# Two layers on one core: the parameters' preparation put behind the first Gram matrix, and one unit's work instead of two beside the second

## The chip, the cores and the metric

The kernel runs on one core of a Trainium2 chip. The metric is the device time of one execution in microseconds (us): here the median of three runs. Everything is in float32.

## What is computed

The input x has the shape 16 x 32 x 128 x 128 (samples, channels, rows, columns). Two residual layers follow one another:

```python
x = x + _L0_conv_ref(_gn(x), Wq, Wkv, Wout, bout)      # attention over channels
x = x + _L1_conv_ref(_gn(x), pn_g, ..., k4_bb)         # four small networks on 8 x 8 windows
```

Layer 0 normalises groups of channels (`_gn`), joins eight samples to 256 channels of 16384 positions, projects them to queries, keys and values, and lets channels attend to channels: `sim` is a product over all positions, so that it follows from the 256 x 256 Gram matrix of x. Once the attention matrix is known, the whole layer is one linear map of the channels at each position. There are two groups of eight samples, so two Gram matrices and two maps.

Layer 1 normalises again, cuts 8 x 8 windows and puts them through four `_fastkan` networks:

```python
ln = _layernorm(x, ln_g, ln_b)
basis = jnp.exp(-((ln[..., None] - GRID) / DENOM) ** 2)       # 8 Gaussians
flat = basis.reshape(*basis.shape[:-2], -1)
return flat @ ws.T + jax.nn.silu(x) @ wb.T + bb
```

Two of them run along a window's columns and rows, one on its positions, and the fourth on their sum.

## The kernel before, in words

**Stages.** The work has three stages on the time axis.

1. *Gram matrix of group 0, then of group 1* (`gram_load`, `gram_turn`, `gram_sum`, L610 to L694). Each needs all positions of eight samples. `gram_load` brings x in 16 loads of 2 MB (8 for each group), half of each issued by SP's queue and half by ACT's (L636), into three pairs of buffers for group 0 and two pairs for group 1. A load waits until the turns on the earlier load of its buffers are done (L627). `gram_turn` has 64 steps: two vector transposes on DVE each (L657), four steps to a load, into two alternating tiles R. `gram_sum` has 64 steps: 16 matmuls each, four for each of four pieces b (L683; the trace shows 32 records a step, two to a matmul). Turn m writes the tile that sum m-2 read. Below, "load m", "turn m" and "sum m" count from 0; turn 32 and sum 32 are the first of group 1, turn 63 and sum 63 the last.
2. *Attention* (L696 to L973), once for each group: a chain of about 50 short steps that goes back and forth between PE, DVE and ACT and ends in the map `pt` and some columns. Attention 0 stands beside the second Gram matrix, attention 1 beside the first units. Its products use the projections' weights, which Pool's queue brings in (`projections`, L589 to L605: eight DMAs of 256 KB, then a copy on Pool, L604).
3. *64 units* of 128 x 1024 elements each: 32 of group 0, then 32 of group 1. For a unit, `layer0_norm` applies the map (L1003), takes the mean out (L1018) and takes the variance (L980); `rows_norm` scales (L1051, L1056, L1060, L1064); SP moves the result into a second layout, `move` (L1097), which `norm_a` needs; `norm_a` and `norm_b` normalise for the networks (L436 to L1122), `scale` multiplies (L1139), `seed` takes the first exponentials on ACT (L1148 to L1156), `ladder` makes the other Gaussians, 7 products of 128 x 2048 on DVE for each of two halves a and b (L1168), and `products` multiplies them with the weights (L436, L1204, L1323). `keep` stores a unit's layer-0 result and `load` brings the next x, which has a single buffer (1 MB, both units of a pair, L993).

**What sets the order.** PE, ACT, DVE and SP run their instructions strictly in the order in which the program issues them. That order is made while the program is built, by a small planner (`Flow.run`, L144). Each task is a generator that asks for an engine with a guessed duration (`step("DVE", 0.6)`), for buffers, or for another task's result (`yield "get", ...`). For the steady state the planner has a fixed cyclic order for each engine (`ORDER`, L53 to L74), in which each entry names a task, its step and how many units it lags. While that order isn't able to go on, or where it would be later, tasks outside it (attention, Gram, parameters, projections) are let in by their modelled time. Among these, three names go first where times are equal (`FIRST`, L76). Until the second Gram matrix is found, only units with a number below `AHEAD` may be started by the cyclic order (L77, L199, L208): units 0 and 1 before the change.

**`parameters`** (L486 to L584) prepares the constants of layer 1. Its first step is Pool's: 32 DMAs of 4.5 KB (`st_a`, into a raw tile `sz`, L501), and 8 of 18 KB (`wt_b`, L507) mixed with 16 of 2 KB (`st_b`, L511). Then come 14 steps on DVE and three transposes on PE (L541): L515 to L528 need the columns loaded at the top (L304 to L308), L550 to L570 need `st_a` (its two halves one after the other), L572 needs `wt_b`, L576 and L577 need `st_b`. `rows_norm` of unit 0 waits for all of it (L1047), and so do the seeds' columns and the products' weights. Pool issues its DMAs in order, at the top of the program first the 40 small ones of the columns (L304 to L308), then `parameters`, then `projections`.

Of the kernel before, what the change touches and what calls it, by code (L numbers as in the profile page):

```python
# [73 lines left out]
}  # L74

FIRST = {"attention", "projections", "parameters"}  # L76
AHEAD, UNTIL = 2, ("gram", 1)  # L77
TURNS = 7


def step(engine, us, *take, lag=None):


    return engine, us, take, LAG if lag is None else lag


class Flow:
# [22 lines left out]
    def put(self, key, value, late=0.0):  # L110
        self.found[key] = (value, self.now + late)
# [128 lines left out]
def conv_preact_kernel(  # L240
# [75 lines left out]
    def column():  # L316
        used[0] += 1
        return vec[:, used[0] - 1 : used[0]]

    eps, one, ones_n = column(), column(), column()  # L320
# [123 lines left out]
    def layers():  # L444
        with ExitStack() as es:
# [39 lines left out]

            def parameters():  # L486

                raw, = yield step("POOL", 40.0, "sz")
                back_t = raw[:, 0:384].rearrange("p (k q m) -> p k q m", k=3, q=4)
                st_a = [  # L490
                    raw[:, 384 + k * NT * 16 : 384 + (k + 1) * NT * 16].rearrange("p (t n) -> p t n", t=NT)
# [97 lines left out]
            def projections():  # L589

                qk, wv_raw, wo, low, mid = yield step("POOL", 5.0, "ad_r", "z", "sz", "att", "u")
                qk = qk.rearrange("p l t w -> p (l t w)").rearrange("p (i k n) -> p i k n", i=2, k=KK)
                wq, wk = qk[:, 0], qk[:, 1]
                wv_ = mid[:, 0:1024].rearrange("p (h k c) -> p h k c", h=PAIRS, k=KK)
                wv_raw = wv_raw.rearrange("p (h m s) -> p h m s", h=PAIRS * KK, s=2)
                wo = wo.rearrange("p (h n) -> p h n", h=PAIRS)
                for s in range(2):
                    nc.gpsimd.dma_start(out=wq[s::2], in_=wqT[s * 64 : (s + 1) * 64])
                    nc.gpsimd.dma_start(out=wk[s::2], in_=wkT[s * 64 : (s + 1) * 64])
                for e in range(2):  # L600
                    nc.gpsimd.dma_start(out=wv_[64 * e : 64 * e + 64], in_=wv[:, e::2])
                    nc.gpsimd.dma_start(out=wo[64 * e : 64 * e + 64], in_=woT[:, e::2])
                yield step("POOL", 3.0)
                nc.gpsimd.tensor_copy(wv_raw, wv_.rearrange("p h k (s m) -> p (h k) m s", s=2))  # L604
                put("projections", (wq, wk, wv_raw, wo, low, mid))  # L605
# [4 lines left out]
            def gram_load():  # L610

                half = S // LOAD
                turn = [m % 3 if m < half else m % 2 for m in range(NBP * half)]
                for m in range(NBP * half):
                    if m == 0:
                        ad, yy, u0, u1, d, sd = yield step("SP", 2.6, "ad", "yy", "u", "u", "d", "sd", lag=-2.6)
                        flat4 = lambda t: t.rearrange("p l t w -> p (l t w)")
                        xs = [  # L620
                            [t.rearrange("p (g n) -> p g n", g=4) for t in pair]
                            for pair in ((flat4(ad), flat4(yy)), (u0, u1), (flat4(d), flat4(sd)))
                        ]
                    else:
                        old = [i for i in range(m) if turn[i] == turn[m]]
                        if old:
                            yield "get", ("turned", 4 * old[-1] + 3)  # L627
                        yield step("SP", 2.6, lag=-2.6)
                    bp, j = divmod(m, half)
                    for queue in (nc.sync, nc.scalar):  # L630
                        if queue is nc.scalar:
                            yield step("ACT", 2.6)
                        for r in (0, 1) if queue is nc.sync else (2, 3):
                            for k in range(KK):
                                at = j * LOAD + r * 512
                                queue.dma_start(  # L636
                                    out=xs[turn[m]][k][32 * r : 32 * r + 32],
                                    in_=x_groups[bp, k, :, :, at : at + 512],
                                )
                    put(("xs", m), xs[turn[m]], fl.moved(6.5, 2.6))  # L640

            def gram_turn():


                turned = yield step("DVE", 0.2, "R", "R")
                turned = [t[:, 0 : 4 * KK * (P + 1)].rearrange("p (b n) -> p b n", b=4) for t in turned]
                for t in turned:
                    nc.vector.memset(t[:, :, P], 1.0)
                for m in range(NBP * STEPS):
                    xr = yield "get", ("xs", m // 4)  # L650
                    if m >= 2:
                        yield "get", ("summed", m - 2)
                    yield step("DVE", 1.3)
                    o = slice(128 * (m % 4), 128 * (m % 4) + 128)
                    for k in range(KK):
                        at = k * (P + 1)
                        nc.vector.transpose(  # L657
                            turned[m % 2][:, :, at : at + P].rearrange("p b (g c) -> p g b c", g=4), xr[k][:, :, o]
                        )
                    put(("turned", m), None)  # L660
                    if m == STEPS - 1:
                        give("d")
                        give("sd")
                    put(("xT", m), turned[m % 2])
# [468 lines left out]
            def scale(name, n):  # L1133
                rb = yield "get", (name, "rb", n)
                v = yield "get", (name, "v", n)
                for i in range(2):
                    o = slice(i * RB, (i + 1) * RB)
                    yield step("DVE", 1.14, lag=0.0 if i == 0 else None)
                    TT(v[:, o], v[:, o], flat(rb[i]), ALU.mult)  # L1139
                    give("Y")  # L1140
                put((name, "scaled", n), v)
# [231 lines left out]
            one = lambda name, task: [(name, 0, task)]  # L1373
            every = lambda name, task, units=N: ((name, n, task(n)) for n in range(units))
            with tc.manual_schedule(engines=IN_ORDER):
                fl.run(
                    [
                        one("parameters", parameters()),
                        one("projections", projections()),
                        (("attention", bp, attention(bp)) for bp in range(NBP)),  # L1380
                        one("gram_load", gram_load()),
                        one("gram_turn", gram_turn()),
                        one("gram_sum", gram_sum()),
                        ((f"products_{k}", n, (pair_a if k == "a" else pair_b)(n)) for k, n in both),
                        every("evict_a", evict_a),
                        every("evict_z", evict_z),
                        every("result", result),
                        every("again", again),
                        every("scale_b", lambda n: scale("b", n), N + BACK),
                        every("scale_a", lambda n: scale("a", n)),  # L1390
                        ((f"seed_{k}", n, seed(k, n, par_a if k == "a" else par_b)) for k, n in both),
                        every("norm_b", norm_b, N + BACK),
                        every("norm_a", norm_a),
                        every("silus", silus, N + LATE),
                        every("move_back", move_back),
                        every("move", move),
                        every("rows_norm", rows_norm),
                        every("keep", keep),
                        every("layer0_norm", layer0_norm),
                        every("load", load),  # L1400
                        every("store", store),
                        ((f"ladder_{k}", n, ladder(k, n)) for k, n in both),
                    ],
                    N + max(BACK, LATE),
                )

    layers()


# [78 lines left out]
```

## Time and profile before

| | us |
|---|---|
| median of three runs (2882.24 to 2889.74) | 2883.42 |
| the profiled execution | 2885.47 |
| its span, first to last instruction | 2883.70 |
| PE busy in the span | 2748.3 (95%) |
| DVE busy in the span | 2685.2 (93%) |
| ACT busy in the span | 2518.4 (87%) |
| turn 0 begins (first L657) / sum 0 begins (first L683) | 14.98 / 17.18 |
| sum 31 ends (first Gram matrix) | 118.78 |
| sum 63 ends (second Gram matrix) | 234.25 |
| first ladder product, unit 0 (first L1168) | 246.54 |
| first ladder product of unit 1 / of unit 2 | 295.2 / 360.02 |
| from then on, a unit takes | 39.5 to 39.6 |

A timeline row of the trace gives the start and the length in us, the engine, the line, the operation, the tiles written and read, and in brackets how long the engine was idle before it and what ended that. A row "by stage" gives a window, its length, each engine's busy time with the number of instructions, the clock granted to TensorE as a share of full speed, the mean share of the DMA engines, and the GB/s that they moved. Busy times of PE are modelled, since matmuls overlap.

### The profile page before, as it was taken

Reading aid. Unit: us, or ns where it says so; the run is one execution under the profiler, and the core shown is the slowest. Engines: PE = TensorE matmul, PEld = TensorE weight load, DVE = VectorE, ACT = ScalarE, POOL = GpSimd, SP = SyncE. Lnnn points to the kernel's source line nnn. Section 1 sums busy time; section 2 is a strip of 40 time slices with the busy share of each in tenths; the row PEclk is TensorE's granted clock in tenths of the full one; section 3 lists DMA queues with packets and bytes.
Section 4 is the critical chain, followed back from the end, with each engine's and each line's share of the span. In section 5 each row is a group of like instructions: output and inputs, shape, how many; then the busy total and the mean of one; then the engine's idle time right before and its main releaser. Section 6 shows DMA issues by size and latency. Waiting matters only on the chain.

```text
span 2883.7 us, 100690 instructions
## 1 busy us (share of the span) xinstructions
PE 2748.3 (95%) x45955; PEld 1092.4 (38%) x45955; DVE 2685.2 (93%) x1793; ACT 2518.4 (87%) x2035; POOL 53.8 (2%) x109
## 2 busy tenths in 40 slices
PE   6899899999999999999999999999999999999985
PEld 6774333333333333333333333333333333333321
DVE  4557799999999999999999999999999999999986
ACT  0018699999999999999999999999999999999973
POOL 5200000000000000000000000000000000000000
PEclk9899999999999999999999999999999999999987
DMA  9660233333333333333333333333333333333311
GB/s 223 165 171 28 78 101 107 109 115 104 98 113 99 117 114 110 104 107 109 115 106 94 115 98 117 114 110 104 108 108 115 110 95 111 101 114 113 103 52 38
DMA packets 206152, 311.04 MB, mean 108 GB/s; under 512 B 24480, under 2 KB 156064, under 8 KB 205728
## 3 DMA queue, kind: packets, MB, share of 16 engines
q1 hardware_dynamic: 192512, 285.29, 33.5%
q10 hardware_dynamic: 9504, 16.85, 2.4%
q8 instruction: 362, 5.93, 0.9%
q0 software_dynamic: 3712, 2.46, 0.4%
q14 instruction: 62, 0.51, 0.1%
HBM read 103.18 MB, written 67.11 MB: 59 GB/s over the span
## 4 chain that ended last, share of the span: by engine, by line
PE 64%; DVE 21%; issue 6%; DMA 4%; ACT 3%; SPq 1%; DVEq 0%; POOL 0%; ACTq 0%; POOLq 0%
PE X L436 25%; DVE u L1168 15%; PE X L1204 10%; PE Y L1003 8%; PE Y L1018 4%; PE Y L436 4%; PE X L1323 4%; PE X L683 3%; DVE yc L1139 3%; PE Y L980 2%; PE Y L1122 2%; DVE yy L1056 2%; DMA sz<-in_w 1%; DMA col<-in_cols 1%; SPq L1240 1%
## 5 line engine op out<-in xcount | busy, mean ns | idle before, releaser
L1168 DVE SCALAR_TENSOR_TENSOR u<-R,u 128x2048 f32<-128x2048 f32 x910 | 2042.6, 2285 | 39.0 <-ACT u L1153 15.2
L436 PE MATMUL X<-u,wt_a 32*32 32x512 f32 x16384 | 658.9, 600 | 8.5 <-DVE u L1168 3.6
L436 PE MATMUL X<-u,wt_b 32*32 32x512 f32 x16896 | 640.3, 608 | 14.8 <-ACT u L1153 9.4
L436 PEld LDWEIGHTS X<-u,wt_a 32*32 32x32 f32 x16384 | 302.2, 103 | 282.6 <-issue 138.4
L436 PEld LDWEIGHTS X<-u,wt_b 32*32 32x32 f32 x16896 | 225.6, 103 | 384.0 <-issue 195.6
L1139 DVE TENSOR_TENSOR yc<-yc,Y 128x1024 f32<-128x1024 f32 x260 | 305.2, 1214 | 7.7 <-PE Y L1122 4.8
L1148 ACT ACTIVATE u<-yc,vec 128x2048 f32<-128x2048 f32 x130 | 258.5, 1988 | 29.7 <-DVE yc L1139 25.9
L1003 PE MATMUL Y<-x,pt 128*128 128x512 f32 x512 | 238.4, 609 | 34.7 <-DVE yc L1139 34.7
L1114 ACT ACTIVATE yc<-Y 128x1024 f32<-128x1024 f32 x260 | 250.5, 1017 | 16.6 <-PE Y L436 16.6
L1156 ACT ACTIVATE R<-yc,vec 128x2048 f32<-128x2048 f32 x130 | 259.4, 1995 | 1.3 <-DVE u L1168 0.3
L1150 ACT ACTIVATE R<-yc,vec 128x2048 f32<-128x2048 f32 x130 | 258.8, 1990 | 0.0
L1117 ACT ACTIVATE u<-yc 128x2048 f32<-128x2048 f32 x130 | 247.5, 1904 | 5.1 <-DVE u L1168 2.5
L1153 ACT ACTIVATE u<-u 128x2048 f32<-128x2048 f32 x130 | 247.1, 1901 | 0.0
L683 PE MATMUL X<-R 128*64 128x193 f32 (+3 forms) x2048 | 156.7, 313 | 39.0 <-DVE R L657 38.2
L982 ACT ACTIVATE lr<-Y,vec 128x512 f32<-128x512 f32 (+1 forms) x194 | 131.5, 678 | 45.4 <-PE Y L980 45.4
L683 PEld LDWEIGHTS X<-R 128*64 128x64 f32 x2048 | 145.1, 142 | 56.7 <-DVE R L657 40.8
L1003 PEld LDWEIGHTS Y<-x,pt 128*128 128x128 f32 x512 | 92.7, 191 | 184.7 <-issue 93.7
L980 PE MATMUL Y<-u,e 128*32 128x512 f32 x1040 | 140.5, 606 | 3.3 <-ACT u L1117 3.3
L1232 ACT ACTIVATE ad<-X,col 128x1024 f32<-128x1024 f32 x128 | 134.1, 1097 | 0.9 <-PE X L436 0.7
L1018 PE MATMUL Y<-xh,c 128*128 128x512 f32 x256 | 128.4, 625 | 1.3 <-DVE yc L1139 1.3
L983 ACT ACTIVATE lr<-lr 128x512 f32<-128x512 f32 (+1 forms) x194 | 122.3, 631 | 6.2
L1204 PE MATMUL X<-sd,silu_a 64*64 64x512 f32 x1024 | 126.3, 608 | 0.0
(210 smaller groups left out, 2468.0 us busy)
## 6 DMA issues: line engine op xcount, KB each, us to landing
xh<-xh SPq DMA_DIRECT2D x128, 512.0 KB
d<-yy SPq DMA_DIRECT2D x512, 128.0 KB
ad_r<-ad SPq DMA_DIRECT2D x512, 128.0 KB
x<-in_x SPq DMA_DIRECT2D x32, 1024.0 KB
out<-xh SPq DMA_DIRECT2D x256, 128.0 KB
u<-in_x SPq DMA_DIRECT2D x28, 256.0 KB
u<-in_x ACTq DMA_DIRECT2D x28, 256.0 KB
ad<-in_x SPq DMA_DIRECT2D x14, 256.0 KB
```

Source lines behind the costliest of these rows:

```text
L436: MM(dst(to, g_), lhsT=wt[32 * g_ : 32 * g_ + 32, :], rhs=rhs(g_, (to - turn[g_]) % 4), start=start, stop=stop,)
L683: MM(g[64 * q : 64 * q + 64, k, lo:hi], lhsT=t[:, b, at : at + 64], rhs=t[:, b, lo:hi], start=first, stop=last,)
L1003: MM(xp[:, u, :], lhsT=pts[bp][:, k, kk * P : (kk + 1) * P], rhs=xr[:, k, u * 512 : (u + 1) * 512], start=k == 0, stop=k == KK - 1,)
L1114: ACT(v[:, i * RB : (i + 1) * RB], flat(yt[i]), AF.Identity)
L1117: ACT(sq, v, AF.Square)
L1139: TT(v[:, o], v[:, o], flat(rb[i]), ALU.mult)
L1148: ACT(u, v, AF.Square, bias=bq)
L1150: ACT(up, v, AF.Exp, bias=bp_, scale=2.0)
L1153: ACT(u, u, AF.Exp, scale=-1.0)
L1156: ACT(down, v, AF.Exp, bias=bn, scale=-2.0)
L1168: STT(t, by, BIG, tiles[at[way]], ALU.min, ALU.mult)
L1204: MM(dst(i, f), lhsT=wt(i)[o, o], rhs=rhs(i, o), start=False, stop=False)
```

## The change

```diff
-AHEAD, UNTIL = 2, ("gram", 1)
+AHEAD, UNTIL = 1, ("gram", 1)
...
             def parameters():
 
-                raw, = yield step("POOL", 40.0, "sz")
+                yield "get", "projections"
+                raw, = yield step("POOL", 85.0, "sz")
...
                     [
-                        one("parameters", parameters()),
                         one("projections", projections()),
                         (("attention", bp, attention(bp)) for bp in range(NBP)),
+                        one("parameters", parameters()),
                         one("gram_load", gram_load()),
```

- `parameters` now waits for `projections`: Pool issues the eight 256 KB DMAs and the copy L604 first, then the 56 small DMAs.
- The planner is told 85 us for that step in place of 40, so it puts the DVE and PE steps of `parameters` later in the two queues. In the built program the first stands behind turn 34 (before: behind turn 12) and the last before turn 40 (before: before turn 21), between steps of attention 0.
- The list's order decides between tasks whose times are equal; `parameters` now comes after the attention in it.
- `AHEAD` is 1: until the second Gram matrix is found, the cyclic order starts unit 0 alone. In the built program unit 1's `layer0_norm` and `rows_norm` follow sum 63 on PE (before: all of their matmuls, L1003, L1018, L980 and L1051, stand before sum 63), and three normalising steps of unit 0 (the last of `norm_a`, the last two of `norm_b`) stand before sum 63 instead of behind it.
- No instruction is added or removed. All engines run the same instructions in another order, and from the first ladder product of unit 2 on the order is the same.

## The prediction

> **What bounds the kernel now.** I read the busy times by stage first. The stages are cut at events of the trace: sum 0 begins at 17.2 us, sum 17 ends at 62.6, the DVE's last wait for parameters ends shortly before 89.7, sum 31 ends at 118.8, sum 63 at 234.2, the first ladder product begins at 246.5, that of unit 2 at 360.
>
> ```profile
> core 0: us, PE busy (x) PEld busy (x) DVE busy (x) ACT busy (x) POOL busy (x), PEclk, DMA share, GB/s
> 17.20:62.60 45.40, 44.47 (x579) 41.56 (x579) 27.17 (x64) 0.00 (x0) 23.34 (x48) 1.00 1.07 231
> 62.60:89.70 27.10, 7.00 (x66) 6.16 (x64) 6.97 (x27) 0.00 (x0) 18.28 (x38) 0.72 0.70 170
> 89.70:118.80 29.10, 29.06 (x384) 27.51 (x384) 18.37 (x29) 0.00 (x0) 3.02 (x4) 0.91 0.61 154
> 118.80:234.20 115.40, 114.11 (x1282) 91.94 (x1283) 63.43 (x142) 27.44 (x35) 0.00 (x0) 0.99 0.57 150
> 234.20:246.50 12.30, 8.53 (x38) 3.17 (x37) 7.00 (x12) 8.37 (x8) 0.00 (x0) 0.94 0.40 119
> 246.50:360.00 113.50, 100.65 (x1435) 42.63 (x1434) 91.03 (x111) 79.62 (x73) 0.00 (x0) 0.93 0.18 50
> 360.00:1360.00 1000.00, 986.97 (x17001) 359.79 (x17006) 991.71 (x556) 976.22 (x783) 0.00 (x0) 1.00 0.36 108
> ```
>
> After 360 us PE and DVE are both 99% busy: the change can't help there, nor does it touch it, since the built program's order is the same from there on. So the question is only when unit 2 begins its ladder. Ahead of that, PE is idle for 20 us at 62.6 to 89.7, for nearly nothing in the next 145 us, then for 17 us (12.3 - 8.5 and 113.5 - 100.7). The timeline says what the 20 us are:
>
> ```profile
> 63.30 1.51 DVE L657 STREAM_TRANSPOSE R<-u 128x512 f32<-128x512 f32 x2
> ...
> 73.19 0.31 DVE L550 TENSOR_TENSOR sz<-sz,fac 128x144 f32<-128x144 f32 x1 [8.37 <-DMA sz<-in_w]
> ...
> 76.43 4.56 PE L683 MATMUL X<-R 128*64 128x257 f32 x32 [9.15 <-DVE R L657]
> ...
> 87.78 0.46 DVE L572 TENSOR_TENSOR wt_b<-wt_b,fac 128x288 f32<-128x288 f32 x1 [11.40 <-DMA sz<-in_w]
> ...
> 89.72 10.58 PE L683 MATMUL X<-R 128*64 128x257 f32 x114 [8.73 <-DVE R L657]
> ...
> 98.78 1.27 POOL L604 COPY z<-u 128x1024 f32<-128x1024 f32 x1 [7.33 <-DMA u<-in_wv]
> ```
>
> DVE stands at L550 and L572 until Pool's small DMAs have landed; turns 19 and 20 are queued behind them, sums 19 and 20 behind those. Why these loads are late, in the list of DMA issues (last column: median us to landing):
>
> ```profile
> sz<-in_w POOLq DMA_DIRECT2D x32, 4.5 KB, 7.3
> u<-in_wv POOLq DMA_DIRECT2D x2, 256.0 KB, 7.8
> sz<-in_w POOLq DMA_DIRECT2D x16, 2.0 KB, 2.4
> ```
>
> 4.5 KB take 7.3 us while the Gram loads fill the DMA engines (231 GB/s, share 1.07), and Pool's timeline shows it waiting after every eight or so until an earlier one has landed: 32 DMAs take 39.7 to 70.1, 0.95 us each; the last 24, after the Gram loads had stopped, 70.1 to 86.3, 0.67 each. The waits behind 246.5 us:
>
> ```profile
> PE Y L877 <- DVE u L870: 6.2, 1, 6.2
> DVE pt L896 <- PE Y L886: 5.5, 1, 5.5
> ```
>
> These are steps of attention 1 that stand too close together in the queues.
>
> **What the Trainium skill says.** "DMA: Bandwidth & Descriptors", section "Queues, rings and completion order": every DMA engine goes round the queues with work, a packet from each, so Pool's queue and the two load queues share the same engines. The trace agrees: 7.3 us for 4.5 KB in traffic, 2.4 us for 2 KB in less. It means that 2 MB of projections aren't free beside 2 MB Gram loads. "TensorE: Matmul & The Clock Gate", section "Architectural detail: the array is 16× 32×32, not 1× 128×128": ACT and DVE are strict FIFO; the rows above show turns behind L550. The same page, "HAM oscillation": idle gaps above about 3.4 us lower PE's clock. Here two gaps of 9 us stand in a stage with a granted clock of 0.72, and sum 19 takes 4.56 us where a dense one takes 2.2. That cost goes with the gaps.
>
> **A. The first Gram matrix.** Without DVE's waits, turns and sums would go on at 2.2 us a step (turn 4 at 26.8, turn 8 at 35.6). From sum 17's end at 62.6, 14 sums take 31: sum 31 would end at 93.4. But the loads are next: DMA moved 16.0 MB in the first 70 us (the ten-us windows give 228, 210, 217, 237, 232, 238, 234 GB/s), which is the first x (1 MB), some 0.2 MB of small ones and seven of eight Gram loads. The eighth, 2.1 MB, was held back by the stall, and so the projections' 2.1 MB came in an empty time. Now they compete from about 40 us: 4.2 MB at 234 GB/s are 18 us, so load 7 lands at 88. Turn 28 starts then, and turn 28 plus four sums give 88 + 1.5 + 4 x 2.2 + 0.3 = 98.6. Saved: 118.8 - 98.6 = **20.2** (25.4 if the projections cost nothing; 15 if Pool's DMAs cost twice their bytes).
>
> **B. Beside the second Gram matrix.** PE's work: unit 1's matmuls leave (L1003 3.6, L1018 1.9, L980 1.0, L1051 1.1: -7.6), unit 0's last norm steps (1.1 + 1.0 + 1.1 = +3.2) and the three transposes (3 x 0.33 = +1.0) come: -3.4. The stage was full, 114 of 115.4, because work of unit 1 and the longer runs of sums filled the attention's waits. In the new order:
> - Load 8 can be issued only when turn 27 is done, about 87, and lands 9 us after load 7, about 98: turn 32 is some 2 us late. +2.2.
> - Between L822 and L836 of attention 0 there stood 17 pieces of sums (9.5 us); now 6 (3.3) and a transpose. DVE does in that time L824/L825 0.8, one copy 0.25, both `st_a` steps (0.31 + 1.0 + 0.4 = 1.7 each, from the rows at 61.8 and 73.2), five small operations 0.9, L830 0.5, and hand-overs 0.5: 6.5. PE waits +3.
> - The map's columns L968 and ACT's L1013 take 2.2 us behind L965; the cover falls from seven pieces (4.06) to three (1.7). +0.7.
> - Sums 50 to 55 stand in a row. With two pairs of buffers a load has four steps, 8.8 us, but needs 9.1 and a landing; the last load's SP half also moves behind `move` of unit 0 (5.64 us of issue at L1097). Loads 14 and 15: between 0 and 8, I take +4.
> - **The parameters' loads.** Pool has the columns issued at 40 us; the projections' 2.1 MB share the engines, so I put the copy L604 at 67 (55 to 85; 12 us between issue and copy in the quieter stage before, about twice in full traffic). 32 DMAs at 0.95 and 24 at 0.67 to 0.95 end at 113 to 120. DVE asks for `wt_b` 21 us behind sum 31, about 120: just in time. A late one holds DVE at L572 with turn 39 queued behind it, and sum 39 after that; about 3 us are covered. Between 0 and 10, I take +1.
>
> Sum: -3.4 + 10.9 = +7.5. Sum 63 ends at 98.6 + 115.5 + 7.5 = 221.6 instead of 234.25.
>
> **C. Behind the second Gram matrix.** PE must now run L1003, L1018, L980, L1051 of unit 1, five steps of attention 1 and two matmul groups of unit 2 ahead of the first product, with four short waits (L1018 for ACT's L1013, 0.9; L779 for ACT's row copies, 0.9; L805, 0.5; L1018 again, 1.0). DVE's first ladder product comes behind L1064 of unit 1, about 18 us after sum 63 instead of 12.3. In exchange attention 1 is further, and its L877 and L896 no longer follow their producers directly: 11 of the 17 us of waits there have cover. One new wait: `move` of unit 1 starts only with the first ladder product, so the first matmuls of `norm_a` wait some 2.5 us. PE until unit 2's ladder: before 109.2 busy + 16.6 idle = 125.8; after 109.2 + 7.6 - 3.2 = 113.6 busy + 3.3 + 2.5 + 2.8 (the rest, as before) = 122.2. DVE alone would need only about 18 + 96: two units of 38.6, 14 us of attention, 5 of waits. PE is later, so unit 2 begins at 221.6 + 122.2 = 343.8 instead of 360.0: **-16.2**.
>
> The profiled execution took 2885.47 (span 2883.70); it becomes 2869.3. It stood 2.05 above the median, so the median becomes 2883.42 - 16.2 = **2867**.
>
> **The rivals.**
> 1. *The stalls of B have cover.* If loads and parameters arrive in time (no +2.2, +4, +1) and half the 3 us are hidden, sum 63 ends at 213; PE gives -25, DVE (213 + 114 = 327) up to -33: about **2857**. For it: DMA's share of 0.57 in that stage. Against: the two-buffer loads.
> 2. *The gain is given back.* PE had no slack from 89.7 to 234; with A at -15, B at +12 and C at 0 only some 3 to 7 us are left: about **2878**. For it: each attention step in B loses filler. Against: two 9 us gaps vanish whatever follows.
> 3. *The parameters' loads arrive far too late* (slower). Pool's order puts 56 DMAs behind the copy. If full traffic lets the projections land only at 90 and each DMA takes 1.3 us, `wt_b` is there at 163, DVE stands 40 us at L572 with all turns behind it: -16 + 40 = +24, **2907**. It passes before's time from a landing at 139 on. For it: 7.3 us landings. Against: traffic falls once two pairs of buffers gate the loads, and the same 24 DMAs took 0.67 us each then.
> 4. *It does nothing*: excluded, the built order is different.
>
> **How the numbers follow.** About 0.3% (8.7 us) is what a measurement of this kernel can tell from no change: faster means below 2874.8. The forecast (2860 to 2874) has 0.47, rival 1 0.22, rival 2 0.22 (a fifth of it still below 2874.8), rival 3 0.09. Faster 0.73, same 0.18, slower 0.09. The range from 2851 to 2880 takes in forecast and rival 1 and two thirds of rival 2.
>
> **What would show it.** A right: no wait at L550 or L572 before sum 31, which ends at 95 to 101, DMA at 230 GB/s until then. B right: sum 63 at 216 to 226, PE idle about 10 us in the stage, most before L836 and at the last loads. C right: first ladder product 18 us after it, unit 2's near 344, no wait above 3 us at L877 or L896. Wrong: a wait at L572 of over 5 us (rival 3), or a first Gram matrix that ends after 105, which would mean that the projections delay the loads by more than their bytes.

## The result, and the profile after

Five executions of the changed kernel took 2869.46 us in the median (2865.74 to 2871.14); five of the kernel before, measured beside them, took 2882.24 (2878.46 to 2889.74). The ratio is 0.9951, with an interval of 0.9935 to 0.9968: faster by about 0.5%. Forecast were 2867 and a range of 2851 to 2880. The profiled execution took 2870.64 (span 2868.9).

Its busy times by stage, cut at the same events as before; sum 0 begins at 16.5, sum 31 ends at 97.1, sum 63 ends at 221.9, the first ladder product begins at 241.1, that of unit 2 at 342.1:

```profile
core 0: us, PE busy (x) PEld busy (x) DVE busy (x) ACT busy (x) POOL busy (x), PEclk, DMA share, GB/s
16.50:54.70 38.20, 38.18 (x512) 36.33 (x512) 21.21 (x30) 0.00 (x0) 16.76 (x32) 1.00 1.07 241
54.70:60.30 5.60, 0.06 (x3) 0.02 (x2) 1.50 (x3) 0.00 (x0) 0.00 (x0) 0.96 1.06 262
60.30:97.10 36.80, 36.80 (x512) 34.91 (x512) 23.09 (x33) 0.00 (x0) 23.27 (x46) 0.96 0.95 237
97.10:221.90 124.80, 115.62 (x1289) 92.86 (x1288) 73.38 (x198) 29.98 (x35) 4.88 (x11) 0.93 0.52 127
221.90:241.10 19.20, 16.69 (x56) 8.66 (x57) 6.97 (x23) 6.55 (x12) 0.00 (x0) 0.91 0.25 82
241.10:342.10 101.00, 94.94 (x1410) 39.51 (x1410) 87.75 (x99) 78.62 (x67) 0.00 (x0) 0.95 0.25 71
342.10:1342.10 1000.00, 986.53 (x16967) 359.12 (x16973) 990.79 (x555) 975.02 (x782) 0.00 (x0) 1.00 0.36 108
```

The stage with a clock of 0.72 is gone. In the first Gram matrix PE now stands only in the second row: 5.6 us, with the DMA engines full at 262 GB/s. The stage beside the second Gram matrix, 97.1 to 221.9, has grown from 115.5 to 124.8 us. From unit 2's ladder on a thousand microseconds look as before. Sum 31 ends 21.7 us earlier than before, sum 63 12.4, the ladder of unit 2 17.9.

The timeline at the row of 5.6 us, DVE and then PE (times in front, idle before in brackets):

```profile
55.58 0.71 DVE L658 STREAM_TRANSPOSE R<-u 128x512 f32<-128x512 f32 x1 [3.77 <-DMA u<-in_x]
59.52 2.12 DVE L658 STREAM_TRANSPOSE R<-u 128x512 f32<-128x512 f32 x3 [3.22 <-DMA u<-in_x]
...
60.28 2.19 PE L684 MATMUL X<-R 128*64 128x257 f32 x12 [5.54 <-DVE R L658]
...
61.25 1.26 POOL L605 COPY z<-u 128x1024 f32<-128x1024 f32 x1 [12.40 <-DMA u<-in_wv]
```

Turn 16, the first on load 4, waits for its load: 3.77 for one half and 3.22 for the other. (Lines behind 488 count one higher in the changed kernel.) Pool issued the projections at 38.2 to 45.1, so they travel beside load 4, and the copy comes at 61.3. The steps of `parameters` on DVE wait for nothing any more:

```profile
116.57 0.30 DVE L551 TENSOR_TENSOR sz<-sz,fac 128x144 f32<-128x144 f32 x1
...
119.25 0.31 DVE L551 TENSOR_TENSOR sz<-sz,fac 128x144 f32<-128x144 f32 x1 [0.21 <-issue]
...
121.43 0.45 DVE L573 TENSOR_TENSOR wt_b<-wt_b,fac 128x288 f32<-128x288 f32 x1
```

Before, the waits here were 8.37 and 11.40 us. The DMA issues show the price of the exchange (last column: median us to landing):

```profile
u<-in_wv POOLq DMA_DIRECT2D x2, 256.0 KB, 16.0
...
sz<-in_w POOLq DMA_DIRECT2D x32, 4.5 KB, 6.9
sz<-in_w POOLq DMA_DIRECT2D x16, 2.0 KB, 4.9
wt_b<-in_w POOLq DMA_DIRECT2D x8, 18.0 KB, 4.8
```

A half of `wv` takes 16.0 us instead of 7.8. And the waits of PE beside the second Gram matrix (us in total, times, longest):

```profile
PE Y L436 <- DMA d<-yy: 6.3, 1, 6.3
PE Y L837 <- DVE u L831: 2.1, 1, 2.1
PE X L684 <- DVE X L677: 0.4, 1, 0.4
PE X L684 <- DVE l0c L969: 0.3, 1, 0.3
```

### The profile page after: what moved, and what is told of

Same layout as the page of the kernel before. It is cut to its first block, busy times and chain, and to the rows that moved or that the text cites. A ratio compares the mean times of both kernels' runs of the same rounds, so it can differ in the third digit from the quotient of the medians.

```text
span 2868.9 us, 100690 instructions
## 1 busy us (share of the span) xinstructions
PE 2746.1 (96%) x45955; PEld 1091.5 (38%) x45955; DVE 2685.3 (94%) x1793; ACT 2517.7 (88%) x2035; POOL 53.8 (2%) x109
## 3 DMA queue, kind: packets, MB, share of 16 engines
q8 instruction: 362, 5.93, 0.9%
## 4 chain that ended last, share of the span: by engine, by line
PE 64%; DVE 20%; issue 6%; ACT 4%; DMA 4%; SPq 1%; DVEq 0%; ACTq 0%
PE X L436 25%; DVE u L1169 14%; PE X L1205 10%; PE Y L1004 7%; PE Y L436 4%; PE Y L1019 4%; PE X L1324 4%; PE X L684 3%; DVE yc L1140 3%; PE Y L1123 2%; PE Y L981 2%; DVE yy L1057 2%; DMA u<-in_x 1%; SPq L1241 1%; ACT u L1118 1%
## 5 line engine op out<-in xcount | busy, mean ns | idle before, releaser
L436 PE MATMUL X<-u,wt_a 32*32 32x512 f32 x16384 | 663.8, 605 | 11.2 <-ACT u L1154 4.1
L436 PE MATMUL X<-u,wt_b 32*32 32x512 f32 x16896 | 638.3, 605 | 16.3 <-ACT u L1154 9.4
L436 PEld LDWEIGHTS X<-u,wt_a 32*32 32x32 f32 x16384 | 302.7, 103 | 289.1 <-issue 136.4
L436 PEld LDWEIGHTS X<-u,wt_b 32*32 32x32 f32 x16896 | 224.7, 103 | 384.3 <-issue 194.2
L684 PE MATMUL X<-R 128*64 128x257 f32 (+3 forms) x2048 | 154.4, 312 | 22.8 <-DVE R L658 22.1
L1205 PE MATMUL X<-sd,silu_a 64*64 64x512 f32 x1024 | 124.7, 602 | 0.0
```

The costliest lines, as they stand in the source:

```text
L436: MM(dst(to, g_), lhsT=wt[32 * g_ : 32 * g_ + 32, :], rhs=rhs(g_, (to - turn[g_]) % 4), start=start, stop=stop,)
L684: MM(g[64 * q : 64 * q + 64, k, lo:hi], lhsT=t[:, b, at : at + 64], rhs=t[:, b, lo:hi], start=first, stop=last,)
L1205: MM(dst(i, f), lhsT=wt(i)[o, o], rhs=rhs(i, o), start=False, stop=False)
```

## The experiments

The change has three parts: Pool issues the projections first; the steps of `parameters` on DVE and PE come later; unit 1 begins later. My theory was the prediction's: the gain is that DVE no longer meets late DMAs, the number of units ahead is nearly neutral, and Pool's new order is a price. The rivals: that unit 1's removal does the work, or that Pool's order does.

Here S31 and S63 are the ends of sums 31 and 63, L2 is the first ladder product of unit 2, all from the profiled execution of each kernel; the ratio is to the kernel before on the same chip, with its 95% interval.

| kernel | median us | ratio | S31 | S63 | L2 |
|---|---|---|---|---|---|
| before (first profile) | 2882.24 | 1 | 118.8 | 234.3 | 360.0 |
| changed | 2869.46 | 0.9951 [0.9935, 0.9968] | 97.1 | 221.9 | 342.1 |
| e1, two units | 2866.32 | 0.9940 [0.9928, 0.9953] | 95.6 | 222.3 | 341.7 |
| e2, one unit alone | 2882.23 | 0.9995 [0.9987, 1.0003] | 116.7 | 226.2 | 356.6 |
| e3, parameters first on Pool | 2863.65 | 0.9929 [0.9916, 0.9941] | 92.7 | 204.7 | 335.0 |
| e4, no unit | 2862.97 | 0.9920 [0.9907, 0.9934] | 93.2 | 192.2 | 338.9 |
| e5, first x load later | 2862.50 | 0.9928 [0.9915, 0.9941] | 91.9 | 215.4 | 332.9 |
| e6, e3 with no unit | 2863.46 | 0.9931 [0.9918, 0.9945] | 85.8 | 189.6 | 338.4 |
| e7, e3 with two units | 2863.31 | 0.9929 [0.9916, 0.9941] | 90.3 | 209.9 | 332.6 |
| e8, Pool's order alone | 2899.20 | 1.0049 [1.0036, 1.0061] | 131.2 | 248.9 | 374.7 |
| e9, e3 and e5 | 2861.88 | 0.9923 [0.9908, 0.9938] | 85.9 | 201.7 | 332.7 |
| e10, e7 and e5 | 2860.38 | 0.9912 [0.9900, 0.9925] | 89.3 | 213.5 | 339.3 |
| e11, changed kernel again | 2868.89 | 0.9942 [0.9930, 0.9954] | 98.3 | 223.1 | 340.6 |

Every ratio is uncertain by about 0.13%, nearly 4 us, so only the larger differences in the table are resolved by times; profiles of single executions help with where, less with how much. Even there S31 scatters: changed, e11 and e1 run the same order up to sum 31 and end it at 97.1, 98.3 and 95.6.

**e1: the change with two units ahead.**

```diff
-AHEAD, UNTIL = 1, ("gram", 1)
+AHEAD, UNTIL = 2, ("gram", 1)
```

> The parameters' half of the change alone; two units still begin beside the second Gram matrix. My theory (the gain is the removed wait of DVE in the first Gram matrix, and the number of units is worth a few us either way): sum 31 ends at 97 as with the whole change, the time falls by 12 to 20 us, to about 2867. Rival (the number of units carries the gain, because attention 1 then stands better among the first units): sum 31 still ends at 97, but the time stays within 6 us of before, about 2878.

2866.32, and L2 at 341.7 against 342.1. The parameters' part alone gives all the gain.

**e2: the kernel before with one unit ahead.**

```diff
-AHEAD, UNTIL = 2, ("gram", 1)
+AHEAD, UNTIL = 1, ("gram", 1)
```

> The other half alone: one unit beside the second Gram matrix, the parameters where they were. My theory: DVE waits at L550 and L572 for about 20 us as before, sum 31 ends at about 119, the time is within 6 us of before, about 2881. Rival (the number of units carries the gain): faster by 8 us or more, 2874 or less.

No change in time. S63 comes 8 us earlier, but the work left out of that stage must be done behind it: the stretch from S63 to L2 grows from 125.7 to 130.4. The other rival, that unit 1's removal matters, is out.

**e3: the parameters' DMAs first on Pool again, their steps still late.**

```diff
-                yield "get", "projections"
                 raw, = yield step("POOL", 85.0, "sz")
...
+                        one("parameters", parameters()),
                         one("projections", projections()),
                         (("attention", bp, attention(bp)) for bp in range(NBP)),
-                        one("parameters", parameters()),
```

> The changed kernel, but Pool issues the parameters' 56 DMAs first and the projections behind them, as before the change; the parameters' steps on DVE and PE stay late (from turn 31 on). Theory: what counts is that DVE asks late, and the projections' 2 MB beside the first Gram loads cost the 5.5 us in which sum 16 waited for load 4. Then that wait is gone, sum 31 ends at 91 to 93, and the time is 0 to 6 us below the changed kernel, about 2866. Rival (the order on Pool's queue is what matters, since attention 0 needs the projections early): attention 0 waits for Pool's copy or wk, and the time is 5 us or more above the changed kernel.

S31 at 92.7, as forecast. By stage:

```profile
17.30:92.70 75.40, 74.32 (x1024) 70.99 (x1024) 45.29 (x68) 0.01 (x1) 39.19 (x80) 1.00 1.06 230
92.70:204.70 112.00, 108.86 (x1272) 90.11 (x1273) 72.06 (x195) 19.52 (x28) 5.31 (x9) 0.98 0.62 161
```

PE is idle for 1.1 us in the first Gram matrix and 3.1 beside the second, against 5.6 and 9.2 in the changed kernel. Its ratio lies 0.0013 to 0.0022 below the changed kernel's two (0.9951, and 0.9942 in e11), some 4 to 6 us, and its L2 5.6 to 7.1 us earlier; the intervals of the ratios overlap, so the profile carries this verdict. It isn't Pool's order alone either: with other modelled times the planner also orders the other engines anew from about sum 31 on. Where the second stage's 6 us went can be seen in SP's queue. The changed kernel first:

```profile
182.95 9.61 SPq L1098 DMA_DIRECT2D d<-yy  x8
192.66 2.51 SPq L637 DMA_DIRECT2D u<-in_x  x4
```

and e3:

```profile
175.32 2.29 SPq L636 DMA_DIRECT2D u<-in_x  x4
183.91 5.93 SPq L1097 DMA_DIRECT2D d<-yy  x8
```

In the changed kernel the `move` of unit 0 (`d<-yy`) is issued ahead of the last Gram load's SP half and takes 9.61 us to issue; PE's L436, which reads `d`, waits 6.34 us for it. In e3 the load goes first, the issue takes 5.93, and L436 waits 0.69. (Before, the load went first too, and the issue took 5.64.)

**e4: the change with no unit ahead.**

```diff
-AHEAD, UNTIL = 1, ("gram", 1)
+AHEAD, UNTIL = 0, ("gram", 1)
```

> The changed kernel with no unit at all beside the second Gram matrix. Theory: a unit beside the Gram matrix is worth having, since its chain of norm steps is hidden there, but it costs the 6.3 us in which the first matmuls of norm_a waited for the move of unit 0 beside the last Gram loads, and clock. Without it, that wait is gone, sum 63 ends at about 208 instead of 222, the first ladder product comes some 35 us behind it, and the time is 2 to 8 us above the changed kernel, about 2875. Rival (units beside the Gram matrix cost as much as they bring): within 2 us of the changed kernel.

A miss. The time fell instead of rising: 0.9920 against 0.9951 for the changed kernel. The stretches around S63:

```profile
93.20:192.20 99.00, 98.01 (x1173) 87.13 (x1172) 66.40 (x191) 4.05 (x13) 5.33 (x12) 0.97 0.58 156
192.20:255.80 63.60, 54.93 (x283) 26.26 (x284) 23.08 (x60) 36.64 (x40) 0.00 (x0) 0.90 0.24 75
```

The second Gram matrix needs only 99 us when no unit stands beside it, and S63 comes 16 us earlier than I had put it. The first ladder product then follows 64 us behind, not 35, so it comes later than I had put it, at 255.8 instead of 243; and yet that of unit 2 comes 3.2 us earlier than in the changed kernel. What I had overlooked was another effect of the edit: with no unit started, the first x load (1 MB), the first DMA on SP's queue in the other kernels, moves behind all Gram loads, and sum 0 begins at 13.8 us, not 16.5. That called for e5.

**e5: the change, with the first x load's DMA behind SP's half of the ninth Gram load, and nothing else moved.**

```diff
+            held = []
...
+                    if m == 8:
+                        held.pop()()
...
-                nc.sync.dma_start(out=xr, in_=x_raw[bp, :, :, j * RB : (j + 1) * RB])
+                bring = lambda: nc.sync.dma_start(out=xr, in_=x_raw[bp, :, :, j * RB : (j + 1) * RB])
+                held.append(bring) if n == 0 else bring()
```

> The changed kernel with one DMA moved: the first 1 MB load of x for the units is issued on SP behind the Gram loads for turn 32, not ahead of all of them. All other instructions keep their places on all engines. Without any unit beside the Gram matrix, sum 0 began at 13.8 us instead of 16.5 and unit 2 at 338.9 instead of 342.1. If that gain is this load's place (theory), sum 0 begins at 13.8 here too, sum 31 ends at about 94, and the time is 2 to 4 us below the changed kernel. Rival (the gain came from having no unit beside the Gram matrix): the 3 us are lost again at turn 32, and the time is within 1 us of the changed kernel.

Sum 0 at 13.8 as expected, S31 at 91.9, L2 at 332.9, 9.2 us ahead of the changed kernel's. The median lies 6 to 7 us below the changed kernel's two; the intervals of the ratios just overlap (0.9941 against 0.9935 and 0.9930). Median and profile speak against the rival, that nothing comes of it, without excluding it; the size lies above the 2 to 4 us that I had given it.

**e6 and e7: e3 with no unit and with two units.**

```diff
-AHEAD, UNTIL = 1, ("gram", 1)
+AHEAD, UNTIL = 0, ("gram", 1)
```

> Parameters first on Pool, their steps late, no unit beside the second Gram matrix. Theory: sum 31 ends at 89 to 90 (92.7 with one unit, less 3 for the x load's place), and the number of units stays neutral, so the time is about 2860, 22 to 25 us below before. Rival (no unit was better for a reason of its own): 2857 or less.

```diff
-AHEAD, UNTIL = 1, ("gram", 1)
+AHEAD, UNTIL = 2, ("gram", 1)
```

> Parameters first on Pool, their steps late, two units beside the second Gram matrix. Theory (the number of units is neutral, since a fuller stage leaves less behind it): within 3 us of the same kernel with one unit, about 2864, sum 63 at about 209. Rival: one unit was chosen rightly and two cost 5 us or more.

e7 is the cleanest of all these tests: it differs from the kernel before in one number, 85.0 in place of 40.0. Pool and SP issue everything in the order of before, both units stand beside the second Gram matrix, and only the steps of `parameters` come later, with the steps that make way for them. Its gain of 0.71% is no smaller than that of the whole change (0.49 and 0.58%): the later steps alone are enough.

The ratios are 0.9931 and 0.9929, against 0.9929 for one unit. S63 lies at 189.6, 204.7 and 209.9 for none, one and two units, and none of this is left at the end. e6 came 3.5 us above my figure: its S31 was earlier than expected (x out of the way), but the 3 us were given back by L2. With e1 and e2 this puts what the number of units is worth below what the times resolve. That PE and DVE have the same work to do, before S63 or behind it, is the reason that I see.

**e8: the kernel before with only Pool's order changed.** The guess of 31.8 keeps every other queue's order as it was.

```diff
-                raw, = yield step("POOL", 40.0, "sz")
+                yield "get", "projections"
+                raw, = yield step("POOL", 31.8, "sz")
```

> The kernel before with Pool's order alone changed: the projections' eight DMAs and the copy first, the parameters' 56 DMAs behind them; every instruction of PE, DVE, ACT and SP stays in its place, so DVE asks for the parameters as early as before. Theory: the gain comes from DVE asking late, and Pool's new order by itself costs: st_a and wt_b land 15 to 20 us later (104 to 108 instead of 88), DVE stands at L550 and L572 until then, sum 31 ends at 134 to 140, and the time is 14 to 20 us above before, about 2900. Rival (Pool's order is what gains): no slower than before.

Slower by 0.49%, some 14 us; in the profile L2 is 14.7 us later. DVE's rows, and then PE's:

```profile
78.84 0.31 DVE L551 TENSOR_TENSOR sz<-sz,fac 128x144 f32<-128x144 f32 x1 [16.07 <-DMA sz<-in_w]
...
86.44 0.31 DVE L551 TENSOR_TENSOR sz<-sz,fac 128x144 f32<-128x144 f32 x1 [4.54 <-DMA sz<-in_w]
...
101.34 0.46 DVE L573 TENSOR_TENSOR wt_b<-wt_b,fac 128x288 f32<-128x288 f32 x1 [11.71 <-DMA sz<-in_w]
```

```profile
81.95 4.17 PE L684 MATMUL X<-R 128*64 128x257 f32 x32 [14.20 <-DVE R L658]
...
103.28 6.95 PE L684 MATMUL X<-R 128*64 128x257 f32 x77 [9.86 <-DVE R L658]
```

Sum 31 ends at 131.2, a little ahead of the 134 to 140 expected. This is the mechanism of the prediction's third rival: the parameters land behind the projections, DVE stands in front of them with all turns queued behind. It is real, and it costs 14 us if DVE asks where it asked before. In the changed kernel DVE asks at 116.6 to 125.7, and the last `wt_b` is issued at 103.9.

**e9 and e10: e5's edit on top of e3 and of e7.**

> Parameters first on Pool, their steps late, one unit beside the second Gram matrix, and the first load of x behind the Gram loads for turn 32. Theory (the two gains add, since one is the projections' 2 MB beside the first Gram loads and the other the 1 MB ahead of them): sum 0 at 13.8, sum 31 at 89, unit 2 at about 331, 4 us below the kernel without the moved load: about 2860. Rival (both are the same thing, bytes ahead of load 7, of which only a part is on the path): within 1.5 us of the kernel without the moved load, 2863.

> The same with two units beside the second Gram matrix. Theory (the number of units stays neutral once no move of a unit meets Gram loads): within 2 us of the kernel with one unit, about 2860. Rival: the kernel with two units is the slower one by 4 us or more, as its unit 2 follows the waits of attention 1 (6.2 us at L877).

e9's 32 sums of the first Gram matrix take 72.5 us with PE busy for 72.48 of them: no wait is left to remove there. x's 1 MB now travels beside the second Gram matrix, which takes 115.8 us instead of e3's 112.0; whether the one is the cause of the other no run shows. In time e9 is 1.8 us below e3, between theory and rival. The two-unit e10:

```profile
14.50:89.30 74.80, 73.67 (x1024) 70.38 (x1024) 45.84 (x72) 0.00 (x0) 40.02 (x81) 1.00 1.04 237
89.30:213.50 124.20, 119.64 (x1288) 96.17 (x1287) 70.62 (x189) 27.42 (x35) 5.30 (x8) 0.95 0.62 161
213.50:225.80 12.30, 8.53 (x38) 3.17 (x37) 7.00 (x12) 8.40 (x8) 0.00 (x0) 0.94 0.40 119
225.80:339.30 113.50, 100.74 (x1435) 42.74 (x1434) 91.06 (x111) 79.56 (x72) 0.00 (x0) 0.93 0.18 50
```

It has the best ratio of all, 0.9912. The profile shown is of its slowest execution (2865.19; the median is 2860.38).

**e11: the changed kernel once more,** beside e9 and e10, with no edit.

> The changed kernel itself once more, on the same chip as the two above: about 2869, ratio to before 0.995. If it comes out at 2864 or less, the differences of a few us between the kernels with late parameters are no more than what separates two sessions.

0.9942: the result stands. e10's interval (up to 0.9925) doesn't touch it (from 0.9930), so **e10 beats the kernel before and the changed one**: its median is 8.5 us below the changed one's beside it. That is the change without its edit of Pool's order and without its edit of the units, and with the first x load moved. It is the best of many, though, and can't be told from e9, nor from e3 to e7: all their intervals overlap.

The kernels with late steps form four groups by what Pool issues first and by where x's first load stands. Within a group the order is the same up to sum 31, or all but the same:

| Pool first / first x load | kernels | S31 | ratios |
|---|---|---|---|
| projections / first | changed, e11, e1 | 97.1, 98.3, 95.6 | 0.9951, 0.9942, 0.9940 |
| parameters / first | e3, e7 | 92.7, 90.3 | 0.9929, 0.9929 |
| projections / later | e5, e4 | 91.9, 93.2 | 0.9928, 0.9920 |
| parameters / later | e9, e10, e6 | 85.9, 89.3, 85.8 | 0.9923, 0.9912, 0.9931 |

At sum 31 each of the two is worth 4.4 to 5.6 us, and they add (means 97.0, 91.5, 92.6 and 87.0). In the time they don't: the mean ratios are 0.9944, 0.9929, 0.9924 and 0.9922, so that either alone saves some 4 to 6 us and both together hardly more. That supports e9's rival, but differences of 0.0015 to 0.0022 are at the edge of what these times resolve.

## Why the prediction was right, point by point

**Where the time is.** Right. From unit 2's ladder to the end before took 2523.7 us; the changed kernel took 2526.8 in its first profile and 2523.5 in e11's, the same program. So the 3.1 us that are missing between L2 (17.9 earlier) and the span (14.8 shorter) aren't the change's; it is scatter between executions.

**A, sum 31 at 98.6, saved 20.2.** Measured 97.1, saved 21.7. Right in cause: the projections' bytes delay the Gram loads, and do no more. The place was wrong, and that the size came out is partly luck. I let load 7 and turn 28 pay; load 4 and turn 16 did, 5.5 us, since load 4 travels just when all eight projections have been issued. The Trainium skill's "DMA: Bandwidth & Descriptors", "Queues, rings and completion order", fits: the queues share engines packet by packet, and 2 MB issued from 38.2 to 45.1 us are taken from the load then under way. Behind that the engines moved more than the 234 GB/s of my sum (264 and 244 from 60 to 80 us), and turn 28 was no longer late. So the 5.2 us that the sum took off for load 7 (98.6 - 93.4) weren't lost there, and the 5.5 lost at load 4 weren't in it. e3, with the projections issued behind the parameters' DMAs, ends the stage at 92.7: Pool's order costs about 4.4 us here, and wins nothing.

**B, +7.5, sum 63 at 221.6.** Measured 124.8 - 115.5 = +9.3, at 221.9. The total was near, the terms less so:

| term | forecast | measured |
|---|---|---|
| PE's work, at full clock | -3.4 | -3.4 |
| half clock | not in the sum | +4.9 |
| turn 32 late | +2.2 | 0 |
| before L836 (now L837) | +3 | +2.1 |
| behind the map's columns | +0.7 | 0 |
| loads 14 and 15 / `move` | +4 | +5.7 |
| the parameters' loads | +1 | 0 |

The four waits shown above come to 9.1 of the stage's 9.2 us of idle time. Before had 1.3: 0.6 ahead of L436, and the same 0.4 for the clearing of X and 0.3 for the map's columns as after. So these two are no part of the change, and turn 32 was in time. -3.4 + 4.9 + 2.1 + 5.7 gives the measured 9.3. (Two sums of the prediction are off by 0.2 or less: DVE's list before L836 comes to 6.4, not 6.5, and 2.2 less a cover of 1.7 is 0.5, not 0.7.)

Two terms failed, and that the total held is partly luck: 6.6 us too little for the clock and `move` stand against 4.8 too much in the other four. The fourth wait isn't for a Gram load but for `move` of unit 0, whose issue grew from 5.64 to 9.61 us: the prediction had counted what `move` does to the load, and not that `move` itself could come late. And the clock was left out. PE's busy time rose by 1.5 us although the work fell. The records of the granted clock show half speed at 121.3 to 124.7, 152.0 to 158.9 and 193.0 to 199.8, with PE busy for 13.3 us of it; before, only at 176.7 to 180.1, 3.4 us busy. A step of sums takes 4.24 us in such a stretch (at 155.1) instead of 2.2, the first four L837 3.66 instead of 1.98. If all matmuls take twice as long there, the stretches cost 6.6 and 1.7 us, an estimate of +4.9; without them PE's work comes to 109.0 us, before to 112.4, which is the forecast -3.4. That the waits bring on the half clock is argued, in the last section, from where the stretches lie; no run took one wait alone away.

**The parameters' loads.** Right: "just in time" was about 14 us in time. e8 shows what stood on it.

**C, 122.2 us, unit 2's ladder at 343.8.** Measured 120.2 and 342.1. The ladder began 19.2 behind sum 63 (forecast 18), the four short waits on PE were 1.2, 0.9, 0.4 and 1.2 us (0.9, 0.9, 0.5, 1.0), and the wait for `move` of unit 1 was 2.4 (2.5). PE's idle time was 8.6 as forecast; its busy time, 111.6 instead of 113.6, makes the difference. The wait of 6.2 at L877 is gone and that at L896 is 0.7.

**The rivals.** The first, that the second stage's stalls have cover (2857), fails in the changed kernel; e3, with sum 63 at 204.7, shows that the cover is there once the loads and `move` aren't in each other's way. The second, that the gain is given back (2878), mixed two things: time won by leaving work for later is given back (e2, e6), the time of removed waits is not. The third needs a DVE that asks early (e8). What the prediction didn't see is that of the change's three parts one carries all of the gain (e7), one is neutral as far as the times tell (e2), and one, Pool's order, costs about 5 us at sum 31 and perhaps 4 in the time; it weighed the parts only together.

## What to carry to other kernels

Where an in-order engine waits for late DMAs, try first to move the waiting instruction: here the later DVE steps gave all of the gain (e7), while the reordered queue cost 14 us alone (e8), and pushed its bytes into a stretch where the loads were the bound. Ask of every early DMA who needs it first: 1 MB of x, issued first and first used at 145 us, cost about 5 us by sum 31. Work moved across a barrier, with the same two engines full on both sides, was worth nothing that the times resolve, though the barrier itself moved by 20 us.

## What the runs showed of the hardware that was not expected

- The issue of `move`, the same eight DMAs of 128 KB, took 9.4 to 9.6 us on SP's queue in the three traces in which ACT issued its half of the last Gram load meanwhile (changed kernel, e5, e11), 5.2 to 7.1 in the eight in which it didn't, and 5.1 with no Gram load left (unit 1's in e3). Full DMA engines alone don't explain it: their share was 1.09 during the 5.64 us before, and 0.86 during the 9.61. The cause stays open.
- The DMA engines moved 230 to 262 GB/s at a share above 1.0, by stretch; I took 234 as a fixed ceiling, and it isn't one.
- The half clock keeps to a grid. In all 13 traces the stretches at half clock begin and end on steps of 3.41 us, whose phase differs from trace to trace. Between 20 and 350 us the traces hold 1136 such steps at full clock. Each of the 32 with more than 2.0 us of idle PE is followed by one at half clock. So are 18 of the 19 with no idle time but more than 2.0 us of one-column matmuls (L930 to L935), and none of the 876 with next to no idle time (under 0.2 us) and less than 1.75 us of these. In between both occur. This is what the traces have in common; no run varied it on purpose.

"HAM oscillation" of the Trainium skill's "TensorE: Matmul & The Clock Gate" speaks of gaps above about 3.4 us; here 2.1 us were enough where they fell into one step. The wait before L837 shows it, in the changed kernel (first two rows) and in e5 (last two), where it is spread over two steps and costs no clock:

```profile
117.90:121.31 3.41, 1.30 (x22) 1.12 (x18) 3.02 (x22) 0.00 (x0) 0.00 (x0) 1.00 0.00 0
121.31:124.72 3.41, 3.41 (x4) 1.16 (x4) 2.32 (x6) 0.00 (x0) 0.00 (x0) 0.50 0.35 70
112.26:115.67 3.41, 2.33 (x37) 2.08 (x31) 2.99 (x25) 0.23 (x2) 0.00 (x0) 1.00 0.00 0
115.67:119.08 3.41, 2.28 (x8) 0.95 (x10) 3.26 (x13) 0.00 (x0) 0.00 (x0) 1.00 0.07 12
```

In e1 and e11 the same wait falls into one step, and half clock follows. The half clock at 152.0 to 158.9 in the changed kernel comes right behind 3.2 us of one-column matmuls, without any gap.
